# A two-layer graph network on one core: a 472-wide last query block, and a last tile of rows in whole steps over free PSUM and two queues

## The chip, the cores and the metric

The kernel runs on one core of a Trainium2 chip. The metric is the device time of one execution in microseconds, the median of several runs. Engines: TensorE (PE, its weight loads PEld), VectorE (DVE), ScalarE (ACT), GpSimd (POOL), and SyncE (SP), which here only issues DMAs.

## The reference

N = 3327 nodes with 128 features, and an adjacency matrix of about 0.24% ones plus the diagonal. Two layers, each followed by a residual add and a normalization of the row:

```
# layer 0, graph attention
H = x @ W.T + b;  e = leaky_relu(A * (H@a_s) + A * (H@a_r).T)
att = softmax(where(A > 0, e, NEG), axis=1)
x = layernorm(x + att @ H)
# layer 1, attention in a transposed reading of the projections
q, k, v = ((x @ Wq.T), (x @ Wk.T), (x @ Wv.T)), each reshaped to (128, N, 8)
a = einsum('dnh,dmh->dnm', q, k) * 128**-0.5 + adj + adj
out = einsum('dnm,dmh->dnh', softmax(a, axis=2), v)
x = layernorm(x + out.reshape(N, 1024) @ Wo.T)
```

So layer 1 is 128 attention problems ("heads" below, index d) of 3327 queries by 3327 keys with an inner width of only 8. Adding the adjacency twice multiplies exp(score) by e squared where there is an edge.

## The kernel before

**Tiling.** The heads d are taken in NG = 32 groups of HG = 4; the four sit in the four 32-row strips of TensorE. The queries of a group are cut into NBLK = 7 blocks of WB = 476 columns; 7*476 is 3332, five more than N, so the last block starts at N - 476 = 2851 and computes its first five columns a second time without storing them (`blocks`, c0 = 5). The keys are cut into NT = 26 chunks (25 of 128, one of 127). A block is 26 rounds; 32 groups of 7 blocks make 224 blocks.

**A round.** `scores` (L134) multiplies keys by queries for two half-chunks into PSUM tiles `scb` of two banks. Every third chunk goes to ACT and POOL: exp into SBUF (L1049), then a multiplication by the edge factor (L1050). The others go to DVE and ACT: DVE adds the adjacency (L1052), and ACT takes the exponential in place some rounds later (L883, two half-chunks of 2x476 at once, 1904 elements of tile `e4`). `products` (L853) multiplies the finished chunk by the values and accumulates in the bank `av`, four rounds behind. After chunk 26, DVE copies `av` to `o4` (L862) and four DMAs store it in DRAM as `oT` (L867). PSUM: `pd` has two `scb` tiles, `pe` one, `pv` one bank for `av`, and one `bank` is left for all side work.

**Order.** The order of all five engines is written out by hand, no scheduler changes it. SP's queue carries, in program order, the adjacency tiles `at` (three stretches ahead), the queries, the stores. Stores are put into a list `pend` and issued two rounds later (`issue`, `tick`). Between the rounds `work` and `work_tensor` put in units of side work: the 26 row tiles of layer 0 with the projections for later groups, and `result(t)`, which finishes the 128 rows of tile t once the groups that hold them are done. `result` loads nine rows of `oT` for each row (`load`, L475, L479), transposes them through the one `bank` (`turn`, L485), divides by the sum in the ninth (`divisor`, `divided`, L491, L494), projects with `wo` in steps of 32 columns (`project`, by `by_columns`, L225), adds the residual, normalizes (L511 to L520) and stores (L525).

**The end.** The last tile (t = 25, 127 rows) needs the last block. After the last round the remaining products are issued, `tick(True)` issues the stores, and `finish_to` runs `result(25)` in one piece. Then each engine loads a flag, which decides whether a general second path must run (it does not here).

`_cut(n)` splits rows into a multiple of 16 and the rest (112 and 15 of 127), for the DMAs.

Of the kernel before, what the change touches and what calls it, by code (L numbers as in the profile page):

```python
# [8 lines left out]
F32 = mybir.dt.float32  # L9
# [3 lines left out]
AF = mybir.ActivationFunctionType  # L13
ALU = mybir.AluOpType
# [3 lines left out]
P = 128  # L18
# [29 lines left out]
def kernel(  # L48
# [39 lines left out]
    HG = 4  # L88
    NG = D // HG
# [7 lines left out]
    NBLK = max(2, -(-N // NB))  # L97
    WB = -(-N // (2 * NBLK)) * 2
    blocks = [(min(b * WB, N - WB), b * WB - min(b * WB, N - WB)) for b in range(NBLK)]

    const = ctx.enter_context(tc.tile_pool(name="const", bufs=1))
    dram = ctx.enter_context(tc.tile_pool(name="dram", bufs=1, space=bass.MemoryType.DRAM))
# [30 lines left out]
    def scores(dst, k4, q4, i, r, j, nb, stop=True):  # L133
        nc.tensor.matmul(  # L134
            dst,
            k4[32 * j : 32 * j + H4, i::NT],
            q4[32 * j : 32 * j + H4, :nb],
            start=True,
            stop=stop,
        )  # L140


    def special():
        with ExitStack() as sx, tc.manual_schedule(engines=ALL):
# [320 lines left out]
            def result(t):  # L465
# [51 lines left out]
                def scale():  # L517
# [5 lines left out]
                    for p0, p1 in _cut(r):  # L523
                        issue(
                            lambda p0=p0, p1=p1: nc.sync.dma_start(out[t * P + p0 : t * P + p1, :], z[p0:p1])  # L525
                        )

                assert H == 8

                units = [("x", load), ("w", 14), ("p", lambda: turn(7, 9, 0)), ("p", lambda: turn(5, 7, 2))]  # L530
# [120 lines left out]

            def open_queries(g, b):
                q4 = qp.tile([P, WB], F32R, name="q4b")
                n0 = blocks[b][0]

                def head(j, engine=nc.sync):
                    for again in range(2):
                        engine.dma_start(
                            q4[32 * j + 16 * again : 32 * j + 16 * again + 16, :].bitcast(F32),
                            _ap(qT, (g * HG + j) * N + n0, [[G, 2 * H], [1, WB]]),  # L660
                        )

                return q4, head
# [6 lines left out]
            def want_adj(n):  # L670

                if n >= len(stretches):
                    return
                g, b, m = stretches[n]
                a = adjs[n] = ap_.tile([P, 3, WB], F32, name="at")
                n0 = blocks[b][0]
                cs = stretch[m]
                if n >= RAW and cs[0] in times:
                    nc.sync.dma_start(a[:, 0, :], ftd[b][m])
                    cs = cs[1:]  # L680
                z = where[cs[0]]
                there = sum(i < REST for i in cs)
                parts = [(0, P, there)]
                if there < len(cs):
                    parts = [c + (len(cs),) for c in _cut(FP)] + [(FP, P, there)]
                for p0, p1, k in parts:
                    if k:
                        nc.sync.dma_start(
                            a[p0:p1, z : z + k, :],
                            _ap(adjT, (p0 * NT + cs[0]) * N + n0, [[NT * N, p1 - p0], [N, k], [1, WB]]),  # L690
                        )

            def make_factor(n):
                if n < min(RAW, len(stretches)) and stretch[stretches[n][2]][0] in times:
                    g, b, m = stretches[n]
                    f = adjs[n][:, 0, :]
                    nc.gpsimd.tensor_scalar(f, f, E2 - 1.0, 1.0, op0=ALU.mult, op1=ALU.add)  # L697
                    if g == 0:
                        issue(lambda: nc.sync.dma_start(ftd[b][m], f))


            nc.vector.memset(dens, 1.0)
# [144 lines left out]
            def products(s, i):  # L847
                if s.left == NT:
                    s.av = pv.tile([P, WB], F32, name="av")
                r, e = kr[i], s.e.pop(i)  # L850
                s.left -= 1
                for j in range(HG):
                    nc.tensor.matmul(  # L853
                        s.av[32 * j : 32 * j + 32, :],
                        s.v4[:r, j, i * H1 : i * H1 + 32],
                        e[:r, j, :],
                        start=(s.left == NT - 1),
                        stop=(s.left == 0),
                    )
                if s.left == 0:  # L860
                    o4 = op_.tile([P, WB], F32, name="o4")
                    nc.vector.tensor_copy(o4, s.av)  # L862
                    n0, c0 = blocks[s.b]
                    for j in range(HG):
                        d = s.g * HG + j
                        issue(
                            lambda j=j, d=d: nc.sync.dma_start(  # L867
                                oT[:, d * N + n0 + c0 : d * N + n0 + WB], o4[32 * j : 32 * j + H1, c0:]
                            )
                        )  # L870

# [6 lines left out]
            def exp_late(now):  # L878
                for item in [x for x in late if x[0] <= now]:
                    late.remove(item)  # L880
                    _, s, i, h0, h1 = item
                    e = s.e[i][: kr[i], h0:h1, :]
                    nc.scalar.activation(e, e, AF.Exp, scale=2.0)  # L883


# [42 lines left out]
                main.append(m)  # L928
            main.append([("n", ("counts", 0, 0))] + judge())
            aside.append(("t", ("counts", 0)))  # L930
            results = [((needs[t] + 1) * total + LAG + 6, result(t)) for t in range(NT)]
            marks = {("P", q): 0 for q in range(len(CH))}
            side = {"main": [], "aside": aside, "since": {"main": 0, "aside": 0}, "read": -2}

# [74 lines left out]
            for g in range(NG):  # L1009
                k4, v4, _ = group  # L1010
                for b in range(NBLK):
                    s = Block()
                    s.g, s.b, s.q4, s.k4, s.v4, s.left, s.e, added = g, b, queries[0], k4, v4, NT, {}, {}
                    for n, rnd in enumerate(rounds):
                        at = b * NR + n
                        if n in starts:
# [18 lines left out]
                        for i, h in rnd:  # L1035
                            sc.append((pe if i in times else pd).tile([P, 2, 512], F32, name="scb"))
                            for t in range(2):
                                scores(sc[-1][: kr[i], t, :WB], s.k4, s.q4, i, kr[i], 2 * h + t, WB)
                        work_tensor(g * total + at, n)
                        for (i, h), z in zip(rnd, sc):  # L1040
                            r = kr[i]
                            if i not in s.e:
                                s.e[i] = sp.tile([P, HG, WB], F32, name="e4")
                                added[i] = 0
                            eh = s.e[i][:r, 2 * h : 2 * h + 2, :]
                            added[i] += 1
                            ah = a[:r, where[i], :].unsqueeze(1).to_broadcast([r, 2, WB])
                            if i in times:
                                nc.scalar.activation(eh, z[:r, :, :WB], AF.Exp, scale=2.0)  # L1049
                                nc.gpsimd.tensor_tensor(eh, eh, ah, op=ALU.mult)  # L1050
                            else:
                                nc.vector.tensor_tensor(eh, z[:r, :, :WB], ah, op=ALU.add)  # L1052
                        now = g * total + at
                        exp_late(now)
                        for i, h in rnd:
# [13 lines left out]
                            products(*waiting.pop(0))  # L1069
                        work(g * total + at, n)  # L1070
            exp_late(NG * total + 2)
            while waiting:
                products(*waiting.pop(0))
            tick(True)
            finish_to(None, NG * total + LAG + 6)


    def load_rows(engine, dst, src):
# [374 lines left out]
```

## Time and profile before

| | |
|---|---|
| median of 3 runs (lowest to highest) | 10106.43 us (10104.61 to 10107.84) |
| the profiled execution's own time | 10105.34 us |
| its span in the trace | 10103.5 us |
| TensorE clock granted, mean | 0.996 |
| busy: PE, ACT, DVE, POOL | 98%, 99%, 93%, 91% |
| from one block's copy L862 to the next, at 4015 to 4282 us | 267.1 us for six |
| last copy L862 | 10076.17 us |

In the lines of groups that follow, a row names the source line, the engine, the operation, the output and inputs with their shape, the count, then the busy time in us and the mean of one in ns, and last the idle time of the engine before it with what ended it. In a timeline the first two numbers are start and duration in us, and brackets hold the idle time before it. Instructions of one engine overlap at their ends, so durations may add up to more than the time.

### The profile page before, as it was taken

How to read it: one execution, taken by the hardware profiler on the slowest of the kernel's cores; microseconds unless marked ns; L12 is line 12 of the kernel's file. 1: busy time of each engine (PE TensorE's matmuls, PEld its weight loads, DVE VectorE, ACT ScalarE, POOL GpSimd, SP SyncE). 2: the span in 40 equal slices, each digit the busy share in tenths (PEclk: the TensorE clock that was granted, in tenths of full speed). 3: DMA queues.
4: the chain of work that ended last, by engine and by line, in shares of the span. 5: the costliest groups of instructions: out<-in, count | busy, mean ns of one | idle time of the engine just before them, and what ended most of it. 6: DMA issues, size and time to landing. Idle time of an engine off the chain costs nothing.

```text
span 10103.5 us, 212078 instructions
## 1 busy us (share of the span) xinstructions
PE 9915.1 (98%) x81971; PEld 3840.4 (38%) x81971; DVE 9371.2 (93%) x11596; ACT 9978.5 (99%) x8352; POOL 9212.9 (91%) x4416
## 2 busy tenths in 40 slices
PE   8999999999999999999999999999999999999998
PEld 3333333333333333333333333333333333333333
DVE  7999999999999999989999999999999999998887
ACT  7999999999999999999999999999999999999998
POOL 7999999999999999989999999999999999998997
PEclk8999999999999999999999999999999999999999
DMA  7655555655555655655555555555555555555553
GB/s 204 199 171 172 173 169 173 179 172 167 176 160 177 180 158 175 179 164 175 168 167 175 181 176 166 159 175 176 175 173 165 163 176 176 174 158 170 165 166 120
DMA packets 1183645, 1730.06 MB, mean 171 GB/s; under 512 B 131527, under 2 KB 1171105, under 8 KB 1178527
## 3 DMA queue, kind: packets, MB, share of 16 engines
q1 hardware_dynamic: 1178700, 1713.92, 56.4%
q8 instruction: 644, 10.55, 0.4%
q14 instruction: 378, 3.10, 0.1%
q10 hardware_dynamic: 3923, 2.50, 0.1%
HBM read 1612.00 MB, written 103.95 MB: 170 GB/s over the span
## 4 chain that ended last, share of the span: by engine, by line
PE 78%; ACT 13%; DVE 4%; issue 2%; POOL 2%; DMA 1%; SPq 0%; ACTq 0%; DVEq 0%; POOLq 0%
PE av L853 40%; PE scb L134 33%; ACT e L883 7%; ACT e L1049 6%; PE bank L225 4%; DVE e L1052 2%; POOL e L1050 2%; DVE o L862 1%; DMA at<-in_adjT_dram 0%; DMA at<-ftd 0%; PE bank L485 0%; POOL at L697 0%; DVE ot L494 0%; DMA a<-in_adjT_dram 0%; DVE w L292 0%
## 5 line engine op out<-in xcount | busy, mean ns | idle before, releaser
L1050 POOL TENSOR_TENSOR e<-e,at 128x952 f32<-128x952 f32 x4032 | 8967.8, 2237 | 804.3 <-ACT e L1049 736.4
L1052 DVE TENSOR_TENSOR e<-scb,at 128x952 f32<-128x952 f32 (+1 forms) x7616 | 8419.5, 1145 | 640.2 <-PE scb L134 327.4
L883 ACT ACTIVATE e<-e 128x1904 f32<-128x1904 f32 (+2 forms) x4256 | 6883.5, 1623 | 4.4 <-DVE e L1052 3.9
L853 PE MATMUL av<-e,v4b 128*32 128x476 f32 x46592 | 5878.6, 573 | 40.2 <-DVE o L862 27.7
L134 PE MATMUL scb<-q4b,k4b 32*128 32x476 f32 (+1 forms) x23296 | 4344.6, 592 | 106.9 <-ACT e L1049 34.2
L134 PEld LDWEIGHTS scb<-q4b,k4b 32*128 32x128 f32 (+1 forms) x23296 | 2529.8, 295 | 4779.0 <-issue 2637.5
L1049 ACT ACTIVATE e<-scb 128x952 f32<-128x952 f32 x4032 | 3876.4, 961 | 65.6 <-PE scb L134 57.0
L853 PEld LDWEIGHTS av<-e,v4b 128*32 128x32 f32 x46592 | 1057.0, 108 | 1067.2 <-issue 615.0
L225 PE MATMUL bank<-hsb,w 128*32 128x129 f32 (+1 forms) x5200 | 278.0, 286 | 0.0
L310 DVE TENSOR_SCALAR_CACHE_REDUCE dump<-a 128x384 bf16<-128x384 f32 (+2 forms) x468 | 247.3, 528 | 0.6
L301 POOL TENSOR_TENSOR w<-w,a 128x384 f32<-128x384 f32 (+3 forms) x225 | 207.2, 921 | 0.1
L292 DVE TENSOR_SCALAR w<-trow,er 128x129 f32<-128x129 f32 x650 | 201.2, 339 | 0.0
L225 PEld LDWEIGHTS bank<-hsb,w 128*32 128x32 f32 (+1 forms) x5200 | 102.4, 108 | 148.4 <-issue 148.4
L862 DVE COPY o<-av 128x476 f32<-128x476 f32 x224 | 146.1, 652 | 8.2 <-PE av L853 7.5
L390 DVE SCALAR_TENSOR_TENSOR lo<-bank,hi 128x128 fp32r<-128x128 f32 (+1 forms) x400 | 116.7, 292 | 13.8
L387 DVE TENSOR_SCALAR hi<-bank 128x128 fp32r<-128x128 f32 (+1 forms) x400 | 112.3, 281 | 0.0
L225 PE MATMUL bank<-wv,x1T 128*32 128x128 f32 x1600 | 85.5, 286 | 4.0 <-DVE vb L411 4.0
L225 PE MATMUL bank<-wo,ot 128*32 128x128 f32 (+1 forms) x1664 | 88.8, 290 | 0.4 <-DVE ot L494 0.4
L225 PE MATMUL bank<-wq,x1T 128*32 128x128 f32 x1600 | 85.2, 285 | 0.0
L225 PE MATMUL bank<-wk,x1T 128*32 128x128 f32 x1600 | 85.2, 285 | 0.0
L485 PE MATMUL bank<-ident,o 128*128 128x128 f32 (+1 forms) x234 | 54.6, 308 | 10.4 <-DMA o<-oT 7.6
L411 DVE COPY vb<-bank 128x128 f32<-128x128 f32 (+1 forms) x200 | 56.3, 281 | 5.8 <-PE bank L225 5.8
(111 smaller groups left out, 652.4 us busy)
## 6 DMA issues: line engine op xcount, KB each, us to landing
at<-in_adjT_dram SPq DMA_DIRECT2D x1736, 476.0 KB
at<-ftd SPq DMA_DIRECT2D x1953, 238.0 KB
k4b<-kT SPq DMA_DIRECT2D x128, 415.9 KB
q4b<-qT SPq DMA_DIRECT2D x1784, 29.8 KB
at<-in_adjT_dram SPq DMA_DIRECT2D x217, 208.2 KB
at<-in_adjT_dram SPq DMA_DIRECT2D x56, 714.0 KB
a<-in_adjT_dram SPq DMA_DIRECT2D x50, 504.0 KB
ftd<-at SPq DMA_DIRECT2D x63, 238.0 KB
```

Of the source, the lines that this page charges most:

```text
L134: nc.tensor.matmul(dst, k4[32 * j : 32 * j + H4, i::NT], q4[32 * j : 32 * j + H4, :nb], start=True, stop=stop,)
L225: nc.tensor.matmul(dst[c0:c1], w[:, c0:c1], mov, **kw)
L292: nc.vector.tensor_scalar(w, s["t"][:, :, :T3], e, None, op0=ALU.max)
L301: nc.gpsimd.tensor_tensor(w, w, s["a"][n][:, c0 - i0 : c1 - i0, :r], op=ALU.mult)
L310: nc.vector.tensor_scalar(z, a, float(k), None, op0=ALU.is_equal, op1=ALU.add, accum_out=even[:, t, at : at + 1])
L390: nc.vector.scalar_tensor_tensor(lo[:r, o : o + QW], s["b"][:r, :QW], scale, hi[:r, o : o + QW].bitcast(F32), op0=ALU.mult, op1=ALU.subtract,)
L853: nc.tensor.matmul(s.av[32 * j : 32 * j + 32, :], s.v4[:r, j, i * H1 : i * H1 + 32], e[:r, j, :], start=(s.left == NT - 1), stop=(s.left = ...
L862: nc.vector.tensor_copy(o4, s.av)
L883: nc.scalar.activation(e, e, AF.Exp, scale=2.0)
L1049: nc.scalar.activation(eh, z[:r, :, :WB], AF.Exp, scale=2.0)
L1050: nc.gpsimd.tensor_tensor(eh, eh, ah, op=ALU.mult)
L1052: nc.vector.tensor_tensor(eh, z[:r, :, :WB], ah, op=ALU.add)
```

## The change

The block list gets a second form, `exact`: the seventh block is LW = 472 wide and starts at N - 472 = 2855, with one column (c0 = 1) computed twice. Every tile keeps its width of 476, and every instruction and DMA of the main path takes the first w columns of each row.

`result(25)` is replaced by three functions. `load_first` reserves tiles and loads `x1row`; it is called before the last products. `load_last` loads `o` over two queues. `at_the_end` transposes the sums into the one bank and the eight heads into a `pd` tile of two banks, divides four heads at a time, projects with whole matmuls into a `pe` tile, and stores over two queues. The four stores of the last `oT` alternate between SP and ACT.

```
+    LW = -(-(N - (NBLK - 1) * WB) // 2) * 2
+    exact = [(b * WB, 0, WB) for b in range(NBLK - 1)] + [(N - LW, (NBLK - 1) * WB - N + LW, LW)]
...
+                def at_the_end():
+                    b = pd.tile([P, 2, 512], F32, name="scb").rearrange("p a (b c) -> p (a b) c", c=P)
+                    rd, ot, st = s["rd"], s["ot"], bg1.tile([P, 12], F32, name="st")
+                    c = bank()
+                    nc.tensor.transpose(c[:, :r], s["o"][:r, H, :], ident[:r, :r])
+                    for h in range(H):
+                        nc.tensor.transpose(b[:, h, :r], s["o"][:r, h, :], ident[:r, :r])
+                    nc.vector.reciprocal(rd[:, :r], c[:, :r])
+                    for h in range(0, H, 4):
+                        nc.vector.tensor_tensor(
+                            ot[:, h : h + 4, :r],
+                            b[:, h : h + 4, :r],
+                            rd[:, :r].unsqueeze(1).to_broadcast([P, 4, r]),
+                            op=ALU.mult,
+                        )
+                    y = pe.tile([P, 2, 512], F32, name="scb")[:, 0, :]
+                    for h in range(H):
+                        whole(y[:, :D], ot[:, h, :], wo[:, h, :], r, start=(h == 0), stop=(h == H - 1))
+                    z = y[:r, 256 : 256 + D]
+                    nc.vector.tensor_tensor(z, y[:r, :D], s["x"][:r], op=ALU.add)
+                    nc.vector.bn_stats(st[:r, 0:6], z)
+                    nc.vector.bn_aggr(st[:r, 6:8], st[:r, 0:6])
+                    for f in rsqrt(s, lambda: st[:r, 7:8], r):
+                        f()
+                    w = bg1.tile([P, D], F32, name="x1")
+                    nc.vector.tensor_scalar(
+                        w[:r], z, st[:r, 6:7], s["root"][:r, 1:2], op0=ALU.subtract, op1=ALU.mult
+                    )
+                    for (p0, p1), engine in zip(_cut(r), (nc.sync, nc.scalar)):
+                        engine.dma_start(out[t * P + p0 : t * P + p1, :], w[p0:p1])
+                def load_first():
+                    s["rd"] = bg1.tile([P, P], F32, name="x1T")
+                    s["ot"] = bg1.tile([P, H, P], F32, name="ot")
+                    s["x"] = bg1.tile([P, D], F32, name="x1row")
+                    for p0, p1 in _cut(r):
+                        nc.sync.dma_start(s["x"][p0:p1], x1d[t * P + p0 : t * P + p1, :])
+                def load_last():
+                    s["o"] = bg1.tile([P, H1, P], F32, name="o")
+                    for (p0, p1), engine in zip(_cut(r), (nc.sync, nc.scalar)):
+                        engine.dma_start(
+                            s["o"][p0:p1], _ap(oT, (t * P + p0) * D, [[D, p1 - p0], [G, H1], [1, D]])
+                        )
+                if t == NT - 1:
+                    return load_first, together(load_last, at_the_end)
...
-                        s.av[32 * j : 32 * j + 32, :],
+                        s.av[32 * j : 32 * j + 32, : s.w],
                         s.v4[:r, j, i * H1 : i * H1 + 32],
-                        e[:r, j, :],
+                        e[:r, j, : s.w],
...
-                    e = s.e[i][: kr[i], h0:h1, :]
+                    e = s.e[i][: kr[i], h0:h1, : s.w]
                     nc.scalar.activation(e, e, AF.Exp, scale=2.0)
...
-            results = [((needs[t] + 1) * total + LAG + 6, result(t)) for t in range(NT)]
+            results = [((needs[t] + 1) * total + LAG + 6, result(t)) for t in range(NT - 1)]
+            end = result(NT - 1)
...
-                                scores(sc[-1][: kr[i], t, :WB], s.k4, s.q4, i, kr[i], 2 * h + t, WB)
+                                scores(sc[-1][: kr[i], t, :w], s.k4, s.q4, i, kr[i], 2 * h + t, w)
...
-                            eh = s.e[i][:r, 2 * h : 2 * h + 2, :]
+                            eh = s.e[i][:r, 2 * h : 2 * h + 2, :w]
...
             exp_late(NG * total + 2)
+            finish_to(None, NG * total + LAG + 6)
+            end[0]()
             while waiting:
                 products(*waiting.pop(0))
-            tick(True)
-            finish_to(None, NG * total + LAG + 6)
+            for k, p in enumerate(pend):
+                p[1](nc.scalar if k % 2 else nc.sync)
+            pend.clear()
+            end[1]()
```

The loads of the queries, of `at` and of its stored factors, the factor's own store, and the copy and store of `o4` are cut to w columns in the same way.

More of the change, by code (lines that the diff above doesn't have):

```diff
@@ L653, in open_queries @@
                 q4 = qp.tile([P, WB], F32R, name="q4b")
-                n0 = blocks[b][0]
+                n0, _, w = exact[b]
                 def head(j, engine=nc.sync):
@@ L658, in head @@
                         engine.dma_start(
-                            q4[32 * j + 16 * again : 32 * j + 16 * again + 16, :].bitcast(F32),
-                            _ap(qT, (g * HG + j) * N + n0, [[G, 2 * H], [1, WB]]),
+                            q4[32 * j + 16 * again : 32 * j + 16 * again + 16, :w].bitcast(F32),
+                            _ap(qT, (g * HG + j) * N + n0, [[G, 2 * H], [1, w]]),
                         )
@@ L675, in want_adj @@
                 a = adjs[n] = ap_.tile([P, 3, WB], F32, name="at")
-                n0 = blocks[b][0]
+                n0, _, w = exact[b]
                 cs = stretch[m]
                 if n >= RAW and cs[0] in times:
-                    nc.sync.dma_start(a[:, 0, :], ftd[b][m])
+                    nc.sync.dma_start(a[:, 0, :w], ftd[b][m][:, :w])
                     cs = cs[1:]
@@ L688, in want_adj @@
                         nc.sync.dma_start(
-                            a[p0:p1, z : z + k, :],
-                            _ap(adjT, (p0 * NT + cs[0]) * N + n0, [[NT * N, p1 - p0], [N, k], [1, WB]]),
+                            a[p0:p1, z : z + k, :w],
+                            _ap(adjT, (p0 * NT + cs[0]) * N + n0, [[NT * N, p1 - p0], [N, k], [1, w]]),
                         )
@@ L695, in make_factor @@
                     g, b, m = stretches[n]
-                    f = adjs[n][:, 0, :]
+                    w = exact[b][2]
+                    f = adjs[n][:, 0, :w]
                     nc.gpsimd.tensor_scalar(f, f, E2 - 1.0, 1.0, op0=ALU.mult, op1=ALU.add)
                     if g == 0:
-                        issue(lambda: nc.sync.dma_start(ftd[b][m], f))
+                        issue(lambda: nc.sync.dma_start(ftd[b][m][:, :w], f))
             nc.vector.memset(dens, 1.0)
@@ L861, in products @@
                     o4 = op_.tile([P, WB], F32, name="o4")
-                    nc.vector.tensor_copy(o4, s.av)
-                    n0, c0 = blocks[s.b]
+                    n0, c0, w = exact[s.b]
+                    nc.vector.tensor_copy(o4[:, :w], s.av[:, :w])
                     for j in range(HG):
@@ L866, in products @@
                         issue(
-                            lambda j=j, d=d: nc.sync.dma_start(
-                                oT[:, d * N + n0 + c0 : d * N + n0 + WB], o4[32 * j : 32 * j + H1, c0:]
+                            lambda engine=nc.sync, j=j, d=d: engine.dma_start(
+                                oT[:, d * N + n0 + c0 : d * N + n0 + w], o4[32 * j : 32 * j + H1, c0:w]
                             )
@@ L1013, in special @@
                     s.g, s.b, s.q4, s.k4, s.v4, s.left, s.e, added = g, b, queries[0], k4, v4, NT, {}, {}
+                    w = s.w = exact[b][2]
                     for n, rnd in enumerate(rounds):
@@ L1044, in special @@
                                 added[i] = 0
-                            eh = s.e[i][:r, 2 * h : 2 * h + 2, :]
+                            eh = s.e[i][:r, 2 * h : 2 * h + 2, :w]
                             added[i] += 1
-                            ah = a[:r, where[i], :].unsqueeze(1).to_broadcast([r, 2, WB])
+                            ah = a[:r, where[i], :w].unsqueeze(1).to_broadcast([r, 2, w])
                             if i in times:
-                                nc.scalar.activation(eh, z[:r, :, :WB], AF.Exp, scale=2.0)
+                                nc.scalar.activation(eh, z[:r, :, :w], AF.Exp, scale=2.0)
                                 nc.gpsimd.tensor_tensor(eh, eh, ah, op=ALU.mult)
                             else:
-                                nc.vector.tensor_tensor(eh, z[:r, :, :WB], ah, op=ALU.add)
+                                nc.vector.tensor_tensor(eh, z[:r, :, :w], ah, op=ALU.add)
                         now = g * total + at
```

## The prediction

> **What bounds the kernel now.** I read the page's shares first, then the costliest groups.
>
> ```profile
> PE 9915.1 (98%) x81971; PEld 3840.4 (38%) x81971; DVE 9371.2 (93%) x11596; ACT 9978.5 (99%) x8352; POOL 9212.9 (91%) x4416
> ...
> L1050 POOL TENSOR_TENSOR e<-e,at 128x952 f32<-128x952 f32 x4032 | 8967.8, 2237 | 804.3 <-ACT e L1049 736.4
> L1052 DVE TENSOR_TENSOR e<-scb,at 128x952 f32<-128x952 f32 (+1 forms) x7616 | 8419.5, 1145 | 640.2 <-PE scb L134 327.4
> L883 ACT ACTIVATE e<-e 128x1904 f32<-128x1904 f32 (+2 forms) x4256 | 6883.5, 1623 | 4.4 <-DVE e L1052 3.9
> L853 PE MATMUL av<-e,v4b 128*32 128x476 f32 x46592 | 5878.6, 573 | 40.2 <-DVE o L862 27.7
> ...
> L1049 ACT ACTIVATE e<-scb 128x952 f32<-128x952 f32 x4032 | 3876.4, 961 | 65.6 <-PE scb L134 57.0
> ```
>
> Four engines are nearly full, but ScalarE is the one that never waits: 4.4 us before L883 and 65.6 before L1049 in the whole run. The busy shares by window (columns: length, then busy of PE, PEld, DVE, ACT, POOL, granted clock, DMA share, GB/s) say the same of six ordinary blocks:
>
> ```profile
> 4015.20:4282.30 267.10, 263.76 (x2142) 101.34 (x2142) 252.56 (x319) 266.89 (x223) 244.67 (x115) 1.00 0.59 177
> ```
>
> ACT 266.89 of 267.10. The chain of waits credits PE with 78%, yet a busy PE includes matmuls held up by score banks that ACT has not emptied; I take ACT as the limit. One block is 267.10/6 = 44.5 us. The timeline of ACT alone gives the rate at which it accepts instructions (start to start, not duration, since they overlap):
>
> ```profile
> 4034.53 0.96 ACT L1049 ACTIVATE e<-scb 128x952 f32<-128x952 f32 x1
> 4035.39 1.79 ACT L883 ACTIVATE e<-e 128x1904 f32<-128x1904 f32 x1
> 4037.07 0.95 ACT L1049 ACTIVATE e<-scb 128x952 f32<-128x952 f32 x1
> ```
>
> 0.86 us after 952 elements, 1.68 after 1904: 0.82/952 = 0.86 ns an element at most. The two lengths of L883 (992 and 1791 ns in the group list by form) give 0.84. I use 0.84.
>
> After the last block comes a tail of about 33 us on one chain. Its timeline:
>
> ```profile
> 10076.17 0.65 DVE L862 COPY o<-av 128x476 f32<-128x476 f32 x1 [4.41 <-PE av L853]
> 10076.85 1.36 SPq L867 DMA_DIRECT2D oT<-o  x4
> 10079.13 0.96 SPq L475 DMA_DIRECT2D o<-oT  x2
> 10080.13 0.86 SPq L479 DMA_DIRECT2D x1row<-x1d  x2
> ...
> 10083.74 1.08 PE L485 MATMUL bank<-ident,o 127*128 127x127 f32 x4 [7.62 <-DMA o<-oT]
> 10084.85 0.97 DVE L491 RECIPROCAL x1T<-bank 128x64 f32<-128x64 f32 x2 [8.03 <-PE bank L485]
> ...
> 10089.46 3.64 PE L225 MATMUL bank<-wo,ot 128*32 128x128 f32 x64 [0.38 <-DVE ot L494]
> 10093.16 0.30 DVE L511 TENSOR_TENSOR bank<-bank,x1row 127x128 f32<-127x128 f32 x1 [3.76 <-PE bank L225]
> ...
> 10097.29 0.80 SPq L525 DMA_DIRECT2D out_dram<-x  x2
> ```
>
> Nothing lies beside these steps, so each us removed there is a us of the end.
>
> **Part 1, the narrower block.** N = 3327 = 6*476 + 471, so only the seventh block of each of the 32 groups narrows: 4 columns of 476, or 0.84%. Per block ACT loses 26 chunks x 4 heads x 4 columns = 416 elements: 416 x 0.84 ns = 0.35 us, times 32 = 11.2 us. That is the gain where ACT alone limits. It may not get all of it: when a projection unit runs beside the loop, DVE is full too. At 4033 to 4038 its four additions (4.50 us with overlap) and the pair hi, lo (0.28 + 0.29) fill the 5.06 us of three rounds. DVE's slope is (415 - 281)/128 = 1.05 ns an element (L494, 256 against 128 wide), it loses 17 chunks x 16 x 1.05 = 0.29 us a block, 9.1 us in all. The two ends being near, I take 10.3. PE would lose about 26 x 4 columns x (0.94 + 0.60 us)/476 = 0.34 us a block and POOL, with 2.24 us of work every 2.53, has slack; neither stops it. The ceiling is everything shrinking by 0.84%: 44.5 x 0.0084 x 32 = 12.0 us.
>
> The same edit makes the operands pieces of a wider row: L883 gets 4 x 472 where it had 1904 in one run, L1050 2 x 472. No group of this shape exists before. Near rows: ACT's L411 writes 128x512 as 64 runs of 8 in 0.58 to 0.61 us, L389 writes 512 in one run in 0.60; so ACT pays nothing for breaks. POOL's L301 works on three runs of 128 in 954 ns and two in 655: 2.34 ns an element, and L1050's one run costs 2237/952 = 2.35. I take 0; bounds -1 to +15 us. The loads have the same packets, 1888 bytes instead of 1904, at a DMA share of 0.59: nothing. The order of the instructions in the loop does not change, on SP's queue either.
>
> **Part 2, the tail**, step by step from the copy L862 at 10076.83.
> - Stores of oT: four issues on SP take 1.36 us, the last starts at about 10077.9 and all have landed at 10079.03 by the chain. With two on SP and two on ACT the last starts at about 10077.3 (an ACT issue took 0.41 to 0.65 us in the prologue). ACT has nothing behind them: its exponentials ended at 10074.3. Gain 0.6 (0.4 to 0.65).
> - Load of o: 112 and 15 rows go out together, not 0.45 us apart, and the 63.5 KB of x1row no longer share the engines, worth 0.19 us at the 337 GB/s seen at 10081.5. The x1row issues move ahead of the last products, 0.86 us on an SP queue that has issued its last adjacency load and waits 26.2 us for L862; nobody is behind them. Gain 0.5 (0.3 to 0.7).
>  Here the Trainium skill (DMA: Bandwidth & Descriptors, Issuing engines are not separate DMA queues) speaks against more: DMAs from different engines run on the same 16 engines, only issue time is saved. The landing took 4.03 us from the second issue, of which some 1.9 is 635 KB at 337 GB/s. If two queues halved that, I would book 1.4; by the rule, 0.5. No run here shows it yet; the engines already stood at a DMA share of 1.12, so I follow the rule.
> - Transposes, division, projection. Before, from 10083.74 to 10093.14: 9.4 us. After, counted from the landing: nine transposes back to back, 0.44 for the first and (1.08 - 0.44)/3 = 0.213 for each more, end at 2.14. The reciprocal of 127 (0.97 as two halves, at most that as one) runs under them. The first division waits for all eight: 508 elements, 281 + 380 x 1.05 = 0.68 us, to 2.85; the second hides under the first four heads. Then eight whole matmuls, two records each, 16 records. Their price depends on the clock:
>
> ```profile
> 24.00:29.00 5.00, 4.51 (x38) 4.13 (x37) 3.12 (x12) 3.90 (x20) 0.00 (x0) 1.00 0.84 308
> ...
> 10089.40:10093.20 3.80, 3.64 (x64) 2.88 (x64) 0.04 (x2) 0.00 (x0) 0.00 (x0) 0.50 0.01 2
> ```
>
>  At 24 to 29 us, clock 1.00, sixteen whole records of L183 took 2.40 us, so the projection would fall from 3.64 to 2.4. But the tail's clock is 0.50. The skill (TensorE: Matmul & The Clock Gate, What's actually happening) says that about 3.4 us of idling halves the clock and about as much work is needed to raise it; the tail's 7.6 us wait does that, and 5.7 us of broken and 3.7 us of unbroken work did not undo it. The wait stays over 6 us after the change. At half clock a record of 128 columns costs at least the transposes' 0.213 (same width, same clock), with its load of weights perhaps 0.28: 3.6 to 4.7 us with the last one's end. I take 3.75. So 32-column steps against whole ones gain nothing here; the gain is in the transposes no longer waiting for one bank. End at 2.88 + 3.75 = 6.6 instead of 9.4: gain 2.8 (1.8 to 4.1, the last with a full clock).
> - The thirteen DVE steps from L511 to L520 stay, 4.1 us. Stores of out: SP issues one DMA, not two (0.80 to 0.39), ACT the other. After its issue SP still loads the flag and branches, and is ready at 10101.5; ACT's same steps took 3.4 us before and fit under SP's. Gain 0.4.
>
> Tail: 0.6 + 0.5 + 2.8 + 0.4 = 4.3 us (2.9 to 5.9).
>
> **Sum.** The profiled execution took 10105.3 us for a span of 10103.5. 10105.3 - 10.3 - 4.3 = 10090.7; the median of the runs is 1.1 above that execution, so 10091.8, 0.14% below 10106.4. A measurement of this kernel tells about 0.2% (20.2 us) from no change, so this is "same".
>
> **Rivals.**
> - The loop gives nothing, only the tail does: if DVE or PE waits for something that does not scale with the columns. For it: PE and ACT are chained by a single score bank for L1049. Against it: that chain's parts scale too. 10106.4 - 4.3 = 10102. Chance 0.07.
> - More than 20.2 us: the loop's ceiling of 12.0, the tail's 5.9 with the clock raised, and 2 us and more of scatter or of shorter waits at block boundaries (69.3 us of weight loads wait for L862 in all). 10085. Chance 0.09.
> - Slower: ACT, the bound, stalls at every break of a row. Extra breaks: per block 15 long L883 x 3 and 4 short ones x 1 = 49, in 32 blocks 1568. At 14.6/1568 = 9.3 ns a break everything is lost; at 25 ns the loop adds 39 us and the time is 10131. Against it the 64 runs of L411. Chance 0.03 over +0.2%.
> - The likeliest, 0.81: 10092, its own range 10087 to 10096.
>
> Faster by over 0.2%: 0.09; slower: 0.03; between: 0.88. Range: from 10086.5 (nearly the full ceilings) to 10101 (nearly no loop gain).
>
> **What would show it.** Right: the seventh block of a group 0.3 to 0.37 us shorter than the others by the copies of L862's successor; the long exponentials about 13 ns shorter; nine transposes near 2.1 us; whole records over 0.2 us apart at clock 0.50; the o load landing after more than 3 us. Wrong: equal blocks; exponentials above 1791 ns in the narrow block; a tail clock of 1.00; ACT's DMA issues over 1 us.

## The result, and the profile after

The changed kernel takes 10093.58 us in the median of 22 runs (10090.90 to 10099.94) against 10106.65 us of the kernel before (22 runs, 10103.43 to 10109.39): a ratio of 0.9987 with a 95% interval of 0.9982 to 0.9993. That is 13.1 us less: under 0.2%, but the interval stays clear of 1. The profiled execution's span is 10090.1 us, against 10103.5.

The page's shares and groups of the kernel after, to be held against those of before (line numbers have moved: L1105 is the old L1050, L1107 the old L1052, L936 the old L883, L906 the old L853, L1104 the old L1049):

```profile
PE 9904.1 (98%) x81923; PEld 3839.3 (38%) x81923; DVE 9357.3 (93%) x11592; ACT 9969.7 (99%) x8352; POOL 9204.1 (91%) x4416
...
L936 ACT ACTIVATE e<-e 128x1904 f32<-128x1904 f32 (+2 forms) x4256 | 6875.6, 1621 | 2.3 <-DVE e L1107 1.7
L906 PE MATMUL av<-e,v4b 128*32 128x476 f32 x46592 | 5870.3, 572 | 42.7 <-DVE o L916 27.2
```

ACT still has almost no idle time. The groups kept apart by form show what the narrow block does to one instruction:

```profile
L936 ACT ACTIVATE e<-e 128x1904 f32<-128x1904 f32 x2880 | 5159.5, 1791 | 1.2 <-DVE e L1107 0.8
...
L936 ACT ACTIVATE e<-e 128x1888 f32<-128x1888 f32 x480 | 852.1, 1775 | 1.1 <-DVE e L1107 0.9
```

The exponential over four pieces of 472 takes 1775 ns, 16 less than the 1791 of one piece of 1904 (13 were expected). So breaks in a row cost ScalarE nothing here, and the slower rival has no footing.

From here on the trace is split at the last copy out of the accumulator (L862 before, L916 after): what precedes it is the loop, what follows is the tail. The loop ends at 10066.31 instead of 10076.17, the tail takes 10090.1 - 10066.31 = 23.8 us instead of 27.3. The tail's timeline after:

```profile
10066.31 0.65 DVE L916 COPY o<-av 128x472 f32<-128x472 f32 x1 [4.37 <-PE av L906]
10066.99 0.64 SPq L920 DMA_DIRECT2D oT<-o  x2
10067.00 0.74 ACTq L920 DMA_DIRECT2D oT<-o  x2
10069.00 0.34 SPq L573 DMA_DIRECT2D o<-oT  x1
10069.31 0.35 ACTq L573 DMA_DIRECT2D o<-oT  x1
10073.38 0.45 PE L536 MATMUL bank<-ident,o 127*128 127x127 f32 x1 [7.11 <-DMA o<-oT]
...
10073.62 1.90 PE L538 MATMUL scb<-ident,o 127*128 127x127 f32 x8
...
10076.30 3.78 PE L186 MATMUL scb<-wo,ot 128*127 128x128 f32 x16 [0.78 <-DVE ot L541]
10080.17 0.30 DVE L551 TENSOR_TENSOR scb<-scb,x1row 127x128 f32<-127x128 f32 x1 [3.34 <-issue]
...
10084.30 0.32 SPq L561 DMA_DIRECT2D out_dram<-x  x1
```

| step of the tail | before, us | after, us | gain | forecast |
|---|---|---|---|---|
| copy to first transpose | 7.57 | 7.07 | 0.50 | 1.1 |
| transposes, division, projection | 9.42 | 6.79 | 2.63 | 2.8 |
| add to the store's issue | 4.13 | 4.13 | 0 | 0 |
| the issue to the end of the span | 6.21 | 5.80 | 0.41 | 0.4 |

(First transpose: 10083.74 and 10073.38. Sum of the gains 3.54.)

### The profile page after: what moved, and what is told of

The parts are those of the page before. It is cut to its first block, busy times and chain, and to the rows that moved or that the text cites. A ratio compares the mean times of both kernels' runs of the same rounds, so it can differ in the third digit from the quotient of the medians.

```text
span 10090.1 us, 211982 instructions
## 1 busy us (share of the span) xinstructions
PE 9904.1 (98%) x81923; PEld 3839.3 (38%) x81923; DVE 9357.3 (93%) x11592; ACT 9969.7 (99%) x8352; POOL 9204.1 (91%) x4416
## 4 chain that ended last, share of the span: by engine, by line
PE 79%; ACT 12%; DVE 4%; issue 2%; POOL 2%; DMA 1%; ACTq 0%; DVEq 0%; SPq 0%; POOLq 0%
PE av L906 40%; PE scb L137 33%; ACT e L936 6%; ACT e L1104 6%; PE bank L228 4%; DVE e L1107 2%; POOL e L1105 2%; DVE o L916 1%; PE bank L488 0%; DMA at<-ftd 0%; POOL at L750 0%; DVE ot L497 0%; DMA at<-in_adjT_dram 0%; DVE w L295 0%; DVE root L220 0%
## 5 line engine op out<-in xcount | busy, mean ns | idle before, releaser
L1105 POOL TENSOR_TENSOR e<-e,at 128x952 f32<-128x952 f32 (+1 forms) x4032 | 8958.8, 2235 | 803.1 <-ACT e L1104 729.1
L1107 DVE TENSOR_TENSOR e<-scb,at 128x952 f32<-128x952 f32 (+1 forms) x7616 | 8407.8, 1143 | 644.7 <-PE scb L137 333.6
L936 ACT ACTIVATE e<-e 128x1904 f32<-128x1904 f32 (+2 forms) x4256 | 6875.6, 1621 | 2.3 <-DVE e L1107 1.7
L906 PE MATMUL av<-e,v4b 128*32 128x476 f32 x46592 | 5870.3, 572 | 42.7 <-DVE o L916 27.2
L1104 ACT ACTIVATE e<-scb 128x952 f32<-128x952 f32 (+1 forms) x4032 | 3872.4, 960 | 66.4 <-PE scb L137 56.7
L906 PEld LDWEIGHTS av<-e,v4b 128*32 128x32 f32 x46592 | 1056.9, 108 | 1068.2 <-issue 611.0
L916 DVE COPY o<-av 128x476 f32<-128x476 f32 (+1 forms) x224 | 145.8, 651 | 7.3 <-PE av L906 6.5
L228 PE MATMUL bank<-wo,ot 128*32 128x128 f32 x1600 | 85.2, 285 | 0.0
L488 PE MATMUL bank<-ident,o 128*128 128x128 f32 x225 | 52.0, 304 | 0.0
```

Of the source, the lines that this page charges most:

```text
L228: nc.tensor.matmul(dst[c0:c1], w[:, c0:c1], mov, **kw)
L906: nc.tensor.matmul(s.av[32 * j : 32 * j + 32, : s.w], s.v4[:r, j, i * H1 : i * H1 + 32], e[:r, j, : s.w], start=(s.left == NT - 1), stop=( ...
L916: nc.vector.tensor_copy(o4[:, :w], s.av[:, :w])
L1104: nc.scalar.activation(eh, z[:r, :, :w], AF.Exp, scale=2.0)
L1107: nc.vector.tensor_tensor(eh, z[:r, :, :w], ah, op=ALU.add)
```

## The experiments

The first four split the change into its parts and test the tail, the next keep TensorE warm in the tail and repeat, and the last ask what sets the pace of the loop. "Period" is the time from one block's copy to the next. The kernels with one queue, with 32-column steps and with blocks cut to 440 columns were executed once each, so they are read in their traces alone.

**The narrow block alone.** The old last tile is put back:

```
-                if t == NT - 1:
-                    return load_first, together(load_last, at_the_end)
...
+            results = [... for t in range(NT)]
...
             while waiting:
                 products(*waiting.pop(0))
...
+            tick(True)
+            finish_to(None, NG * total + LAG + 6)
```

> The narrow seventh block with the old last tile. Theory (the two parts are independent, and add up): the last copy out of the accumulator comes about 9.9 us earlier than in the kernel before (10076.2 to about 10066.3) and the tail behind it keeps its 27.4 us, so the span is near 10093.7. Rival (part of the 9.9 us comes from the moved stores and loads at the end or is scatter between executions): the last copy comes less than 7 us earlier.

Its timeline:

```profile
10065.02 0.65 DVE L914 COPY o<-av 128x472 f32<-128x472 f32 x1 [4.36 <-PE av L904]
```

The last copy comes 11.1 us earlier than before, the tail takes 10092.3 - 10065.02 = 27.3 us, as before. Median 10096.60 us, 8.5 less than the 10105.11 of the kernel before beside it; ratio 0.9992 (0.9983 to 1.0000).

**The new last tile alone.** `exact = [(n0, c0, WB) for n0, c0 in blocks]`, so all blocks are 476 wide.

> Blocks of 476 as before, the new last tile alone. Theory: the last copy stays at 10076 within 2 us of scatter and the tail falls from 27.4 to 23.8 us, a span near 10100. Rival (the new tail needs the narrow block, or its 3.5 us were scatter): tail above 26 us.

```profile
10073.58 0.65 DVE L916 COPY o<-av 128x476 f32<-128x476 f32 x1 [4.41 <-PE av L906]
```

The tail takes 10097.6 - 10073.58 = 24.0 us: that part holds, and the parts add up. But the last copy comes 2.6 us earlier than before with a loop that does the same work; the 2 us allowed for scatter were too few. Median 10101.43 us, 3.7 less than 10105.11; ratio 0.9996 (0.9988 to 1.0005). By the medians the parts add up to 12.2 us, but the interval of this part alone holds no change at all, so the sizes are taken from the traces.

That scatter matters for the size of the loop's gain, so I looked for it in the periods of all traces. It sits in three places. Among the first seven blocks, the fourth to the sixth differ by up to 1.3 us each between executions. The first two seventh blocks (the 7th and the 14th of 224) take 50.5 to 54.0 and 49.3 to 50.3 us in the kernels with whole work, without regard to the change. And the last three blocks together take 140.1 us in the profile of before and 137.7 here with the same work, and 137.2 or 139.8 among the narrow kernels. Elsewhere blocks of the same width agree to 0.07 us (0.24 in the third block). I didn't find what makes the last three blocks fall one way or the other. The median period of the seventh blocks is free of it: 44.53 us before and 44.50 here, against 44.28 to 44.30 in all seven traces whose narrowing is that of the change alone (the repeats below included). With 0.02 us more in the sixth blocks, whose period holds the first rounds of the narrow one, that is some 0.25 us a block or 8 us in 32 groups. The 9.9 us between the two first profiles are these 8 us and most of the 2.4 to 2.9 us by which the last three blocks fell differently, less small losses early on.

**One queue for the tail.** All DMAs of the last tile go over SP:

```
-                    for (p0, p1), engine in zip(_cut(r), (nc.sync, nc.scalar)):
+                    for (p0, p1), engine in zip(_cut(r), (nc.sync, nc.sync)):
...
-                p[1](nc.scalar if k % 2 else nc.sync)
+                p[1](nc.sync)
```

> The changed kernel, but all DMAs of the last tile issued by SP alone. Theory (two queues save issue time alone): from the last copy to the first transpose 7.5 us instead of 7.1, and 0.4 us more at the stores of the result, so a tail of 24.6 us. Rival (two queues also carry the data faster): the first transpose comes 8.3 us or more after the last copy.

```profile
10065.91 0.65 DVE L916 COPY o<-av 128x472 f32<-128x472 f32 x1 [4.37 <-PE av L906]
10066.59 1.36 SPq L920 DMA_DIRECT2D oT<-o  x4
10068.82 0.96 SPq L573 DMA_DIRECT2D o<-oT  x2
...
10073.33 0.44 PE L536 MATMUL bank<-ident,o 127*128 127x127 f32 x1 [7.47 <-DMA o<-oT]
...
10084.25 0.81 SPq L561 DMA_DIRECT2D out_dram<-x  x2
```

7.42 us from the copy to the first transpose, against 7.07 with two queues and 7.57 in the kernel before; a tail of 10090.3 - 10065.91 = 24.4 us. So of the 0.50 us gained at this step, 0.35 come from the second queue and 0.15 are left for the early load of `x1row`; at the store the second queue gives 0.3. This agrees with the Trainium skill (DMA: Bandwidth & Descriptors, Issuing engines are not separate DMA queues), on which the prediction rested: the second queue saves issue time. Had two queues also carried the data faster, going back to one would have taken the rival's 8.3 us or more, not 7.42.

**The projection in 32-column steps.** `by_columns` in place of `whole` in the new tile, the rest as changed.

> The changed kernel with the projection of the last tile in steps of 32 columns again (64 records), all else as changed. Theory (at half clock both forms cost the same, the gain of the new middle of the tail is in the transposes that no longer wait for one bank): the projection takes 3.6 to 3.9 us as with whole steps, tail 23.8 us within 0.3. Rival (whole steps carry part of the 2.65 us): the projection takes 0.8 us longer or more, tail 24.6 us.

```profile
10081.58 3.64 PE L228 MATMUL scb<-wo,ot 128*32 128x128 f32 x64 [0.78 <-DVE ot L541]
```

3.64 us against 3.78, with a tail of 10095.3 - 10071.58 = 23.7 us: whole steps are no gain here, they cost 0.14 us. The 2.63 us of this step come from the transposes and divisions, 5.72 us from the first transpose to the first projection before (10083.74 to 10089.46) and 2.92 after (10073.38 to 10076.30), of which the projection and the gap behind it give back 0.17. They no longer take turns in one bank, and there are fewer and longer divisions; the two were not tried apart.

**Keeping TensorE warm.** Seven matmuls that nobody reads fill TensorE's wait for the load:

```
             pend.clear()
+            hot = bank()
+            for k in range(7):
+                nc.tensor.matmul(hot, wo[:, k % H, :], wo[:, :4, :].rearrange("p h c -> p (h c)"), start=True, stop=True)
             end[1]()
```

> The changed kernel with seven idle matmuls of 512 columns (a product of the output weights with themselves into the free bank, never read) put on TensorE between the last products and the transposes, so that it does not stand still for 7 us. Theory (the tail's matmuls are slow because the clock has fallen to one half while TensorE waited for the load): clock 1.00 at the transposes, nine transposes in about 1.2 instead of 2.1 us, the sixteen records of the projection in about 2.4 instead of 3.8, the tail 21.5 instead of 23.8 us. Rival 1 (the records are slow because of their weight loads or because each waits for DVE): the same 2.1 and 3.8 us. Rival 2 (the idle matmuls run past the landing): the transposes start later than 7.1 us after the last copy.

The busy shares of the stretches of the tail in which TensorE works (columns as before, the clock is the third from the right), first of the changed kernel, the transposes and then the projection:

```profile
10073.35:10076.30 2.95, 2.14 (x10) 1.77 (x10) 1.70 (x3) 0.00 (x0) 0.00 (x0) 0.50 0.00 0
10076.30:10080.10 3.80, 3.78 (x16) 3.48 (x16) 0.54 (x1) 0.00 (x0) 0.00 (x0) 0.50 0.02 4
```

then with the seven matmuls, which run in the stretch of the first row:

```profile
10065.80:10072.87 7.07, 6.15 (x14) 2.46 (x14) 0.65 (x1) 0.00 (x0) 0.00 (x0) 1.00 0.34 94
10072.87:10075.00 2.13, 1.17 (x9) 0.96 (x9) 1.66 (x3) 0.00 (x0) 0.00 (x0) 1.00 0.00 0
10075.00:10077.10 2.10, 2.04 (x16) 1.85 (x16) 0.58 (x1) 0.00 (x0) 0.00 (x0) 1.00 0.00 0
```

The clock stays at 1.00, nine transposes take 1.17 us instead of 2.14, sixteen records 2.04 instead of 3.78. The tail is 10087.2 - 10065.80 = 21.4 us, as the theory said. The idle matmuls end before the load lands, so they delay nothing. Median 10090.81 us, ratio to before 0.9987 (0.9980 to 0.9994).

**Both once more, side by side.** The changed kernel and the warm one, 21 executions each on one chip.

> The changed kernel once more. Theory (the loop's gain is 4 columns x 26 chunks x (1.61 + 0.44) ns = 0.21 us in each of 32 blocks, 7 us, and a gain above it is scatter): the last copy between 10064 and 10072, the tail 23.8 us, the seventh blocks' median 44.29 us. Rival (the 9.9 us of the first profile is the gain): the last copy within 1 us of 10066.3.

> The kernel with the seven idle matmuls once more, beside the changed kernel. Theory: 2.3 us below it in the tail (21.4 against 23.8), and the median of the runs 2 us below it within the scatter of 2 us. Rival (the tail's gain is lost elsewhere, in the flag's branch or in the end of the program): medians equal within 1 us, tail above 23 us.

The changed kernel: 10093.57 us, ratio 0.9988 (0.9981 to 0.9994), last copy at 10067.66, tail 23.9 us, median of the seventh blocks 44.29. The warm kernel: 10091.97 us, ratio 0.9986 (0.9979 to 0.9992), last copy at 10070.73, tail 10091.9 - 10070.73 = 21.2 us. The tail's gain is shown twice. In the runs' medians it is 1.6 us. The two ratios share the runs of the kernel before, so how far their intervals overlap says little; set against each other directly, the 21 times of each differ by 2.1 us in the mean, with a 95% interval of 0.7 to 3.5. So the warm kernel is faster in the time too, by a size that fits the tail. This execution's late last copy is the scatter of above.

**What sets the loop's pace.** Four columns are too few to tell the engines apart, so the seventh block was cut to 440 columns in 25 of its 26 key chunks, for one kind of work after the other. Scores and additions may be cut only where all that reads them is cut too, or it would read what nobody wrote; exponentials in place and products may be cut alone.

```
+            NARROW = 440
+            def width(s, i, kind):
+                return NARROW if s.b == NBLK - 1 and i != order[0] and kind in KINDS else s.w
...
-                        e[:r, j, : s.w],
+                        e[:r, j, :v],                                   # v = width(s, i, "av")
...
-                    e = s.e[i][: kr[i], h0:h1, : s.w]
+                    e = s.e[i][: kr[i], h0:h1, : width(s, i, "late")]
...
-                                scores(sc[-1][: kr[i], t, :w], s.k4, s.q4, i, kr[i], 2 * h + t, w)
+                                v = width(s, i, "scores")
+                                scores(sc[-1][: kr[i], t, :v], s.k4, s.q4, i, kr[i], 2 * h + t, v)
...
```

> The changed kernel, with 25 of the 26 key chunks of every seventh block cut from 472 to 440 columns for scores, additions, exponentials, multiplications and products alike (the first chunk stays whole); 32 queries of that block get sums over one chunk alone, so that part of the result is left out. It magnifies the narrowing eight times. Theory A (ScalarE sets the pace, 0.84 ns an element): 25 x 4 x 32 = 3200 elements less a block, 2.69 us, 86 us in all, the last copy near 9980. Theory B (VectorE sets it, 1.05 ns on 16 chunks): 2.15 us, 69 us in all. Theory C (TensorE sets it, 3.24 ns a column and chunk): 2.59 us, 83 us.

> As the one before, but only ScalarE's exponential in place (16 of the 17 chunks that go over VectorE) is cut to 440 columns; all else stays at 472. The last 32 columns of the block are left without exponential. Theory A (ScalarE alone sets the pace): 16 x 128 elements x 0.84 ns = 1.72 us a block, 55 us in all. Theories B and C: nothing, within 3 us. If several engines are full together: a part of 55 us, and less than half.

> As before, but only the products with the values are cut to 440 columns in 25 of 26 chunks; the last 32 columns of the block then hold one chunk alone. Theory C (TensorE sets the pace): 25 x 32 x 1.97 ns = 1.58 us a block, 50 us in all. Theories A and B: nothing, within 3 us.

> The changed kernel, with both the products with the values and ScalarE's exponentials in place cut to 440 columns (25 and 16 chunks of every seventh block; the last 32 columns hold one chunk alone, so that part of the result is left out); scores, additions and the rest at 472. Theory (TensorE's own work sets the pace, ScalarE follows within 0.3 us a block, so that the products alone gave 0.3 us and the exponentials alone nothing): the products cost (572 - 543)/36 x 2 = 1.61 ns a column and chunk, 25 x 32 x 1.61 = 1.29 us a block less, 41 us in all, the last copy near 10025. Rival (the ring of scores, additions and score banks sets the pace, with DVE in it): not above the 10 us that the products alone gave, the last copy near 10056.

> As the one with narrow products and late exponentials, and VectorE's additions cut to 440 columns too (16 chunks of every seventh block). Full at 472 stay the scores, ScalarE's first exponentials and GpSimd's multiplications. The seventh block's period from copy to copy was 44.29 us at 472, 43.81 with products and late exponentials narrow, 42.72 with everything narrow. Theory (the third that holds the pace is VectorE with its additions, which empty the score banks that TensorE waits for): most of the missing 1.1 us comes with the additions, the period falls to 43.0 us or below. Rival (scores and first exponentials through the single bank of that path hold it): 43.6 us or above.

In the last one, `width(s, i, "scores")` becomes `"adds"` for the addition of VectorE's chunks alone. The two columns of TensorE add up the time from the start of each group of score records, or of product records, to the start of TensorE's next group; the projections between them take another 1.94 us in all rows. All but the last copy are medians over the seventh blocks:

| cut to 440 | period, us | ACT idle in it, us | TensorE on scores, us | TensorE on products, us | last copy |
|---|---|---|---|---|---|
| nothing (the changed kernel) | 44.29 | 0.08 | 17.65 | 24.79 | 10066.3 |
| exponentials in place | 44.29 | 1.04 | 17.76 | 24.68 | 10069.6 |
| products | 44.00 | 0.00 | 18.07 | 24.02 | 10056.3 |
| products, exponentials in place | 43.81 | 0.60 | 18.19 | 23.70 | 10051.0 |
| the same and VectorE's additions | 43.28 | 0.14 | 17.72 | 23.67 | 10038.1 |
| everything | 42.72 | 0.38 | 17.40 | 23.41 | 10010.8 |

The windows of one seventh block (the 147th of all), columns as before. Changed kernel, exponentials cut, products cut, everything cut:

```profile
6593.05:6637.24 44.19, 43.72 (x380) 17.29 (x380) 40.62 (x49) 44.18 (x38) 40.02 (x20) 1.00 0.82 217
```

```profile
6596.92:6641.14 44.22, 43.73 (x380) 17.33 (x380) 40.62 (x49) 43.28 (x38) 40.04 (x20) 1.00 0.80 218
```

```profile
6587.18:6631.08 43.90, 43.17 (x380) 17.62 (x380) 40.62 (x49) 43.90 (x38) 39.89 (x20) 1.00 0.82 222
```

```profile
6554.63:6597.27 42.64, 42.05 (x380) 17.18 (x380) 38.67 (x48) 42.35 (x38) 37.81 (x20) 1.00 0.83 225
```

The second window is the telling one: ACT's busy time falls by 0.9 us, and the block is no shorter. ACT simply stands idle. (Its exponentials in 16 chunks are 1.7 us shorter together; the rest of that shows as neighbours that overlap less.) So theory A falls, and with it the first premise of the prediction. The last copy even came 3.3 us later, which is scatter: the first two seventh blocks took 53.8 and 51.6 us there.

With the products cut, ACT has no idle time left and the gain stops at 0.29 us: ACT's own limit at 472 is near 44.0 us, 0.3 below the period. So ACT is the next limit, close behind. That made TensorE the next candidate. Its slopes come from the groups by form of the kernel with everything cut:

```profile
L912 PE MATMUL av<-e,v4b 128*32 128x476 f32 x38400 | 4808.4, 572 | 36.2 <-DVE o L922 23.2 <-POOL e L1113 11.5 <-DMA at<-ftd 0.6
L137 PE MATMUL scb<-q4b,k4b 32*128 32x476 f32 x19200 | 3678.8, 592 | 93.1 <-ACT e L1112 36.8 <-DMA q4b<-qT 15.4 <-DMA k4b<-kT 4.6
...
L912 PE MATMUL av<-e,v4b 128*32 128x440 f32 x6144 | 723.9, 543 | 1.6 <-POOL e L1113 1.6
L137 PE MATMUL scb<-q4b,k4b 32*128 32x440 f32 x3072 | 592.7, 576 | 15.2 <-ACT e L1112 3.3 <-DVE e L1115 2.3 <-DVE jz L639 0.6
```

A product's record loses 29 ns for 36 columns (0.81 ns a column, two records in turn for a chunk), a score's 16 (0.44). For everything cut that gives 25 x 32 x (1.61 + 0.44) ns = 1.64 us a block, 52.5 us in 32; measured were 55.5 by the last copy. The near fit does not make TensorE's own work the only limit: with products and exponentials both cut, it should have given 41 us, and the last copy came 15.3 us earlier.

Cutting the additions as well brought 0.53 us of the 1.09 then missing. I had set 43.0 us and below for VectorE as the holder, 43.6 and above for the other path; 43.28 lies between.

The columns of TensorE say where the time goes. With products and exponentials cut, TensorE spends 1.09 us less on products, but 0.54 us more on scores that are as wide as before; with the additions cut too, the scores are back at 17.72. The chain of waits shows the same. Here are three rounds of it (start, time on the chain, what), first of the changed kernel, then with products and exponentials cut:

```profile
6598.11 0.53 PE scb L137 x4
6598.64 0.36 PE bank L228 x8
6599.00 0.79 PE av L906 x8
6599.79 0.72 PE scb L137 x4
6600.50 0.93 PE av L906 x8
6601.43 0.78 PE scb L137 x4
6602.21 0.93 PE av L906 x8
```

```profile
6594.12 0.58 PE scb L137 x3
6594.71 0.36 PE bank L228 x8
6595.06 0.74 PE av L912 x8
6595.80 0.77 PE scb L137 x4
6596.57 0.88 PE av L912 x8
6597.45 0.79 PE scb L137 x3
6598.24 0.88 PE av L912 x8
```

In both the chain stays on TensorE: three products, three scores and a projection in the order of the program, 5.03 us and 4.99. The products give up 0.15 us, the scores take back 0.11. So TensorE's work in its order is the path, and what its products save is partly lost at the scores, until the additions, which empty two of the three score tiles, are faster too. The run with narrow additions speaks for a wait of the scores for these banks; how much such waiting a score holds at 472 columns everywhere is not known, as the scores can't be cut alone. For the same reason the last 0.56 us, between the last two rows of the table, are not divided among scores, first exponentials and GpSimd's multiplications. When all kinds of work are cut together, the gain is near TensorE's slopes again, 1.57 us a block against 1.64.

## Why the prediction was right or wrong

**The time** (10091.8 forecast, 10093.6 measured) and its side, within 0.2%, were right, and so were both parts as gains that add up. Two terms were too large, and one premise was wrong. That the sum came within 1.8 us is partly luck: the forecast was 14.6 us, the parts seen in the traces are 8 and 3.5, and the 1.6 us between these and the measured 13.1 have no explanation.

**"ScalarE is the limit" was wrong.** It rested on ACT's lack of idle time, and set the chain's 78% for PE aside. With its exponentials cut ACT stood idle 1.04 us a block and nothing was gained. The 11.2 us worked out from it for the loop did not come. I took 10.3, between ACT's figure and VectorE's 9.1; the loop gave about 8 us by the block periods. The step that failed is the assumption that the gain lies between these two engines' slopes, with TensorE put aside ("neither stops it"). TensorE holds the three rounds of the chain shown above, and its slope is the smallest: the forecast of 0.34 us a block was worked out in proportion from 0.94 and 0.60 us and so counted fixed time as time per column; by the slopes it is 0.21, and the seventh block lost 0.24. The prediction's own sign of being right, a seventh block 0.3 to 0.37 us shorter than the others, failed with it: 44.29 us against 44.45 for the others, and before it was 44.53, longer than they.

**Breaks in rows** cost nothing, as said: GpSimd's multiplications took 2220 ns for 2 x 472 where they took 2237 for 952. The count of 49 breaks a block left out ScalarE's 18 first exponentials; these took 953 ns instead of 961. No cost of the loads shows in the periods.

**The tail**: 3.5 us instead of 4.3. (The prediction's 33 us for it count the last products too, from 10070.5; from the copy it was 27.3.) The middle (2.63 for 2.8) and the store (0.41 for 0.4) were sized well, with the clock at one half, as the row of the old tail had it, and with 3.78 us for the projection against 3.75. By the row from 24 to 29 us alone, at full clock, the projection would have been put at 2.40 us, 1.4 too short; the warm kernel shows such a price to be real once the clock is kept up (2.04 us). Stores and load were forecast at 0.6 and 0.5 us and gave 0.50 together. The prediction let the load land earlier by the whole time saved at the last store's issue; the stores' landing took longer (1.60 us on the chain instead of 1.46), so SP's load left 2.69 us after the copy began instead of 2.96, and ACT's load left 0.31 us behind SP's, not with it.

**The rivals.** The loop gained, so "the tail only" falls; the slower one falls with the 1775 ns. More than 20.2 us did not come, and the clock that it needed was not there.

The measured 13.1 us are 1.6 more than 8 + 3.5. The interval of the ratio, 7 to 18 us, holds both, and the scatter of the last blocks alone is over 2 us, so I don't explain the rest; the repeat, 13.0 us below the kernel before beside it, leaves it open as well.

## What to carry to other kernels

An engine that never waits need not be the limit: in a loop with several engines nearly full, cut one engine's work by some per cent (here 32 of 472 columns) and see whether the time or only its idle time moves, and then whether what one group of instructions saves comes back as time in another. Take slopes from two sizes of the same instruction, not from one size in proportion. In a tail behind a load of several us, price TensorE at the clock the tail really had, and fill its wait with matmuls that nobody reads: 2.3 us of the tail here for seven of them.

## What the runs showed that I had not expected

- Two profiles of the same loop differ by up to 5 us at the last copy (10065.9 and 10070.7 in narrow kernels), nearly all of it in the first 14 and the last three of 224 blocks; a gain of 8 us is read better from the median period of the blocks between.
- Whole projection steps and 32-column steps cost the same at half clock within 0.14 us (3.78 and 3.64).
- The old tail behind the narrow block ran its 64 records in 3.31 us instead of 3.64. The clock rose before they ended: 0.50 from 10078.18 to 10081.01 us, 1.00 from there to 10081.50. So the clock rose 2.8 us into this projection, and in the kernel before not within its 3.64 us.
- When the clock falls differs as much: with TensorE idle, it was 0.50 from 2.2 us after the last copy on in the first trace of the changed kernel, and still 1.00 at 5.2 us in the repeat. The tail took the same time in both (23.8 and 23.9 us), as the wait outlasts either.
